# Graph attention on one Trainium2 core: loading x ahead of the edges' numbers, preparing these on POOL, and reordering node work in the turns and at the end

## The chip, the cores and the metric

The kernel runs on one core of a Trainium2 chip. A core has five engines that the profile names: PE (TensorE, matrix products and transposes, with its weight loads listed as PEld), DVE (VectorE), ACT (ScalarE), POOL (GpSimd) and SP (SyncE, which here only issues DMAs). Each takes its instructions strictly in the order of the program, and semaphores make one wait for another. The metric is the time of one execution on the device in microseconds; lower is better.

## The reference

12,500 nodes with 128 features each, and 212,500 edges sorted by their destination `dst`. With 8 heads of 16 features, cut to what matters:

```python
h = maximum(layernorm(x), 0)
q = (h @ Wq.T + bq); k = (edge_h @ Wk.T + bk); v = (h @ Wv.T + bv)   # 8 heads x 16
qs, qd = q[src], q[dst]
in_m, out_m, diag_m = sum(qs * k), sum(qd * k), sum(qs * qd)          # over 16 features
score = (segment_softmax(in_m * 0.25, dst) + segment_softmax(out_m * 0.25, dst)
         + segment_softmax(diag_m * 0.25, dst)) * distance ** lam
h = segment_sum(score[..., None] * v[dst], dst)
return x + leaky_relu(h @ Wo.T + bo, slope=0.1)
```

Since `v[dst]` is the same for all edges of a node, only the three sums of weighted and unweighted exponentials are needed for each node and head; v is multiplied in afterwards, node by node.

## The kernel before, in words

The function is `ordered_path`. It has three stages, all in one program.

**Preparation** (`prep`). x is loaded whole into `xq` (98 tiles of 128 nodes) by nine DMAs in SP's queue. For each group g of four tiles DVE takes statistics (`statistics`, `scale`), ACT normalizes (`rectify`, L863), PE transposes (L870), ACT copies (`hT`, L872), PE multiplies by Wq (L878), DVE adds bq (L881) and SP stores the result to the table `q_table` (L882). Between groups stand pieces of other work, called from the dictionary `side` at a given g: the edges' numbers (`edges_1` to `edges_4`), the transposes of the other weights (`turn_ws`) and the biases' three-term form (`biases`, L822). The edges' numbers are `src`, `dst` and the edge weights, each as 104 rows of 2,048; they are loaded by POOL's queue (`rows_in`, L608 to L610). From src come the transposed integers `src_i`, by which rows are gathered (PE L749, DVE L750); from dst and the weights come bf16 tables in memory: `fa_d` (marks where a segment starts, and three bf16 terms of the weight, written by `fa_out`, L758), `rel_d` (the node's number within a block, L786) and `ends_d`. These share two buffers tagged `of`. After the groups a loop over `terms_q` splits q into three bf16 terms and stores them as `q3_table` (L898 to L907), while POOL begins to gather. The first nine groups of gathers (`gather`, L656) need all of `q_table`. At the end of the stage some small instructions work out a flag (L954 to L978); what follows waits for it.

**The edge loop.** The edges stand in 416 blocks of 512, cut into five strips. One iteration g handles one block; five iterations s = 0 to 4, one for each strip, make a turn t, and there are 84 turns. In an iteration PE, in this order, computes k for block g+1 (`project`, L1115 and L1117), spreads q of the destinations over block g+1 by a one-hot product (`spread_q`, L1126, into the one buffer `qd_ps`), and transposes the features of block g+2 (`turn`, L1107). ACT copies `qd_ps` (L1128) and the transposed features `eT` (L1109) and makes the one-hots of block g+3 (L1101, L1102). DVE forms the products and sums them to logits (`logits`, L1137, L1138, L1140). POOL gathers q of the sources nine blocks ahead. In fixed steps s the preceding turn is handled: its logits are transposed (s=0), scanned for maxima (s=1), turned into powers (s=2: PE L1182, ACT L1183 to L1188), scanned for sums (s=3, DVE L1194 and L1198), its ends shown (s=4, L1214 to L1218), and the sums of the turn before it are transposed (L1226), gathered to rows (L1239) and stored (L1251). The PSUM tiles of these steps come from one tag, `small`, with three buffers in rotation.

**Node work.** Units of 256 nodes whose sums are complete are handled in pairs, 20 of them, each over four turns, by `nodes_between`, which is called as the last thing in an iteration: sums and x loaded, normalized, divided (`scores`), transposed (`turn`), multiplied by Wv (`project_v`: PE L1049 and L1051, then DVE L1059), and two turns later by Wo (`project_o`: PE L1049 and L1051, ACT L1069, DVE L1070 and L1071), and stored. The remaining nine units, `rest`, are five `Nodes` objects; `begin_rest` loads, normalizes, transposes and multiplies them by Wv during the last iterations, and the loop at the end of the function does what needs the last sums: `scores` (whose first addition, L1032, joins two parts of a unit's sums), L1059, the transposes, `project_o` and the store.

Order is written by hand: `pin` makes an instruction follow the one pinned before it on its engine, so each engine's order is that of the Python calls. Buffers and semaphores do the rest.

```python
        side = {2: edges_1, 5: turn_ws, 6: biases, 8: edges_2, 11: edges_3, 14: lambda: edges_4(0),
                17: lambda: edges_4(1), 20: lambda: edges_4(2)}
```

Of the kernel before, what the change touches and what calls it, by code (L numbers as in the profile page):

```python
# [20 lines left out]
SLOPE = 0.1  # L21
# [451 lines left out]
def ordered_path(ctx: ExitStack, tc: tile.TileContext, flag, x, src, dst, edge_attr, edge_weight,  # L473
# [131 lines left out]
    def rows_in(to, t, q):  # L605

        top, cut = (RW - 1) * RC, 96
        q.dma_start(to[0:cut, :], t[:cut * RC].rearrange("(r c) -> r c", c=RC))  # L608
        q.dma_start(to[cut:RW - 1, :], t[cut * RC:top].rearrange("(r c) -> r c", c=RC))
        q.dma_start(to[RW - 1:RW, :E - top], t[None, top:E])  # L610
# [69 lines left out]
    with tc.tile_pool(name="prep", bufs=1) as prep, \  # L680
# [7 lines left out]
        pin(nc.sync.dma_start(w_in[:, 0, :], Wq))  # L688
        xq = prep.tile([P, NI, F], F32, name="xq")
        LOADS = [0, 2, 4] + list(range(CU, NU + 1, CU))  # L690
        for lo, hi in zip(LOADS, LOADS[1:]):
            nodes_in(xq[:, 2 * lo:2 * hi, :], lo, hi - lo, nc.sync)
            if lo == 0:
                pin(nc.sync.dma_start(bq_all, bq[None, :].to_broadcast([P, F])))
        b_row = prep.tile([1, 3, F], F32, name="b_row")
# [15 lines left out]
        src_r = prep.tile([RW, RC], I32, name="src_r", tag="step")  # L711
        nc.gpsimd.memset(src_r[96:, :], 0)
        rows_in(src_r, src, nc.gpsimd)

        dst_r = prep.tile([RW, RC + 2], I32, name="dst_r")
        nc.gpsimd.memset(dst_r[96:, :], N)
        nc.gpsimd.memset(dst_r[:, 0:1], -1)
        rows_in(dst_r[:, 1:RC + 1], dst, nc.gpsimd)
        pin(nc.gpsimd.dma_start(dst_r[1:, 0:1], dst[RC - 1:(RW - 1) * RC:RC, None]))
        pin(nc.gpsimd.dma_start(dst_r[:RW - 1, RC + 1:], dst[RC:(RW - 1) * RC + 1:RC, None]))  # L720
        weight = prep.tile([RW, RC], F32, name="weight")
        nc.gpsimd.memset(weight[96:, :], 1.0)
        rows_in(weight, edge_weight.rearrange("e o -> (e o)"), nc.gpsimd)
# [39 lines left out]

        def edges_1():
            pin(nc.vector.tensor_copy(src_f, src_r))
            turn_edges(src_f, src_i)

        def edges_2():
            pin(nc.gpsimd.tensor_copy(dst_f, dst_r))
            step = got["step"] = prep.tile([RW, RC + 1], F32, name="step", tag="step")  # L770
            pin(nc.vector.tensor_sub(step, dst_f[:, 1:], dst_f[:, :RC + 1]))
            of = of_tile()
            pin(nc.gpsimd.tensor_scalar(of, step[:, :RC], 0.0, -FAR, op0=ALU.is_gt, op1=ALU.mult))
            fa_out(0, of)

        def edges_3():
            base_c = prep.tile([RW, RB], F32, name="base_c")
            pin(nc.vector.tensor_copy(base_c, dst_f[:, 1:RC + 1:BE]))
            for a in range(RB):
                part = rel[:, a * BE:(a + 1) * BE]  # L780
                pin(nc.vector.tensor_scalar(part, part, base_c[:, a:a + 1], 1.0, op0=ALU.subtract,
                                            op1=ALU.add))
            rel_b = of_tile().rearrange("r (a e) -> r a e", a=RB)
            pin(nc.gpsimd.tensor_copy(rel_b.rearrange("r a (j p) -> r a j p", j=JN),
                                      rel.rearrange("r (a p j) -> r a j p", a=RB, j=JN)))
            pin(nc.sync.dma_start(rel_d.rearrange("(r a) e -> r a e", a=RB), rel_b))  # L786

        def edges_4(c):
            of = of_tile()
            pin(nc.gpsimd.tensor_copy(of, weight))  # L790
            if c < 2:
                pin(nc.vector.tensor_sub(weight, weight, of))
            fa_out(c + 1, of)
# [94 lines left out]
        def terms_q(g):  # L888

            if g < GN:  # L890
                n = len(tiles_of(g))
                q = xq[:, g * JN:g * JN + n, :]
                if g % 3 == 2:
                    q3 = prep.tile([P, JN, 3, F], BF, name="q3", tag="of", bufs=2)
                else:
                    q3 = node.tile([P, JN, 3, F], BF, name="q3", bufs=4)
# [13 lines left out]

        side = {2: edges_1, 5: turn_ws, 6: biases, 8: edges_2, 11: edges_3, 14: lambda: edges_4(0),
                17: lambda: edges_4(1), 20: lambda: edges_4(2)}
# [17 lines left out]
        for g in range(-2, GN):  # L930
# [8 lines left out]
            if g in side:  # L939
                side[g]()  # L940
        for g in range(LOOK):
            gather(g)
        for g in range(AHEAD):
            fetch_edges(g)
        fetch(0)
        for g in range(GN + 1):
            terms_q(g)
            if g % 3 == 2:
                edges_5(g // 3)
# [44 lines left out]
    class Nodes:  # L994
# [59 lines left out]
        def project_v(self, to):  # L1054
            self.product(to, bv3, wv)
            self.weigh(to)
# [8 lines left out]
        def project_o(self, to):  # L1065
            n = self.n
            self.product(to, bo3, wo)
            o, y = self.h[:, :n], self.x[:, :n]
            pin(nc.scalar.activation(o, to[:, :n], AF.Copy, scale=SLOPE))  # L1069
            pin(nc.vector.tensor_max(o, o, to[:, :n]))  # L1070
            pin(nc.vector.tensor_add(y, o, y))  # L1071
# [18 lines left out]
    with tc.tile_pool(name="work", bufs=2) as work, \  # L1090
# [167 lines left out]

        def nodes_between(t, s):
# [5 lines left out]
            if new and even and s == 2:  # L1265
                new.normalize(0, 2)
                new.scores()
# [25 lines left out]
        def begin_rest(at):  # L1293
# [4 lines left out]
            for r, (of, begin) in enumerate(zip(rest, starts)):  # L1298
# [23 lines left out]
        for g in range(end + 2 * S):  # L1322
            s, t = g % S, g // S
            if g < end:
# [94 lines left out]
```

## Time and profile before

| | |
|---|---|
| median of 14 runs | 2898.01 us (2885.97 to 2908.07) |
| the profiled execution | 2887.07 us |
| its span in the profile | 2885.3 us |
| mean granted PE clock | 0.706 |
| busy share PE, DVE, ACT, POOL | 69%, 72%, 58%, 57% |
| first gather (POOL, L656) | at 95.02 us |
| first product of the edge loop's logits (DVE, L1137) | at 153.20 us |
| last L1140 | at 2825.81 us |
| last store issued | at 2878.51 us |

The profile's page gives the busy time of each engine, the span in slices, the DMA queues, the chain that ended last, and groups of instructions by source line, with the idle time of the engine in front of each group and what ended it. Further views list instructions in order of time, the waits by pair of waiting and releasing instruction, and the busy time of each engine in chosen windows. Line numbers in the profile before are those of the kernel before.

### The profile page before, as it was taken

How to read it: one execution, taken by the hardware profiler on the slowest of the kernel's cores; microseconds unless marked ns; L12 is line 12 of the kernel's file. 1: busy time of each engine (PE TensorE's matmuls, PEld its weight loads, DVE VectorE, ACT ScalarE, POOL GpSimd, SP SyncE). 2: the span in 40 equal slices, each digit the busy share in tenths (PEclk: the TensorE clock that was granted, in tenths of full speed). 3: DMA queues.
4: the chain of work that ended last, by engine and by line, in shares of the span. 5: the costliest groups of instructions: out<-in, count | busy, mean ns of one | idle time of the engine just before them, and what ended most of it. 6: DMA issues, size and time to landing. Idle time of an engine off the chain costs nothing.

```text
span 2885.3 us, 36583 instructions
## 1 busy us (share of the span) xinstructions
PE 1982.8 (69%) x10781; PEld 1525.0 (53%) x10781; DVE 2087.3 (72%) x2180; ACT 1665.5 (58%) x3049; POOL 1645.3 (57%) x1716
## 2 busy tenths in 40 slices
PE   5256766766667676767677777776767676777676
PEld 4145555555555555555555555555555555555554
DVE  7757776777777777767776777777767777777775
ACT  5645655555555656556555555565555555656573
POOL 4665666666656556556565555656655556555630
PEclk8657766676777767767776667677667677777677
DMA  6853334334343434343443433443433334433431
GB/s 174 272 157 108 112 116 117 109 115 121 109 118 113 121 104 119 114 116 116 118 116 107 121 112 115 125 114 112 118 105 121 108 115 119 122 108 114 118 90 33
DMA packets 308901, 341.93 MB, mean 119 GB/s; under 512 B 139780, under 2 KB 227609, under 8 KB 308382
## 3 DMA queue, kind: packets, MB, share of 16 engines
q1 hardware_dynamic: 246259, 223.55, 26.0%
q0 software_dynamic: 54448, 112.96, 14.0%
q10 hardware_dynamic: 7984, 3.00, 0.4%
q8 instruction: 86, 1.41, 0.2%
q14 instruction: 124, 1.02, 0.1%
HBM read 308.22 MB, written 31.07 MB: 118 GB/s over the span
## 4 chain that ended last, share of the span: by engine, by line
PE 42%; ACT 24%; another core or an unknown queue 13%; issue 10%; DMA 5%; DVE 3%; POOL 1%; SPq 0%; ACTq 0%; POOLq 0%; DVEq 0%
PE k_ps L1117 15%; PE eT_ps L1107 7%; ACT eT L1109 4%; ACT qq L1128 4%; ACT relb L1101 4%; PE qd_ps L1126 4%; ACT oh L1102 4%; PE w_ps L1239 3%; PE b_ps L1226 3%; PE k_ps L1115 3%; PE d_ps L1214 2%; ACT l L1160 2%; DMA qq<-q_table,src_i 2%; ACT sel L1217 2%
## 5 line engine op out<-in xcount | busy, mean ns | idle before, releaser
L656 POOL DMA_INDIRECT qq<-q_table,src_i x1680 | 1608.4, 957 | 1085.5 <-issue 471.3
L1117 PE MATMUL k_ps<-wk,eT 128*128 128x128 f32 x3360 | 677.8, 364 | 621.6 <-ACT eT L1109 296.3
L1117 PEld LDWEIGHTS k_ps<-wk,eT 128*128 128x128 f32 x3360 | 575.0, 258 | 776.9 <-issue 361.5
L1140 DVE TENSOR_REDUCE lT<-prod 128x96 f32<-128x1536 f32 x420 | 736.3, 1753 | 14.3
L1128 ACT COPY qq<-qd_ps 128x512 f32<-128x512 f32 x420 | 244.7, 583 | 598.2 <-PE qd_ps L1126 187.7
L1137 DVE TENSOR_TENSOR prod<-qq,qd_ps 128x512 f32<-128x512 f32 x420 | 285.8, 681 | 386.3 <-ACT qq L1128 197.7
L1138 DVE TENSOR_TENSOR prod<-qq,k_ps 128x1024 f32<-128x1024 f32 x420 | 510.2, 1215 | 0.0
L1109 ACT COPY eT<-eT_ps 128x512 f32<-128x512 f32 x420 | 247.1, 588 | 348.8 <-remote 250.5
L1107 PE MATMUL eT_ps<-ident,ea 128*128 128x128 f32 x1680 | 359.5, 355 | 6.1 <-DVE found L955 5.6
L1101 ACT ACTIVATE relb<-relb,before 126x512 bf16<-126x512 bf16 x420 | 305.9, 728 | 0.0
L1126 PE MATMUL qd_ps<-win,oh 126*128 126x128 bf16 x1680 | 217.9, 270 | 114.9 <-DVE prod L1137 78.1
L1102 ACT ACTIVATE oh<-relb 126x512 bf16<-126x512 bf16 x420 | 264.5, 630 | 23.0 <-DVE flag L978 9.7
L1107 PEld LDWEIGHTS eT_ps<-ident,ea 128*128 128x128 f32 x1680 | 256.1, 189 | 5.9 <-DVE found L955 5.9
L1126 PEld LDWEIGHTS <-oh 126*128 126x128 bf16 x1680 | 171.3, 125 | 143.7 <-DVE prod L1137 79.9
L1226 PE MATMUL b_ps<-ident,sum 120*128 120x120 f32 x672 | 151.6, 364 | 89.2 <-ACT l L1160 63.1
L1115 PE MATMUL k_ps<-b,ones 3*128 3x512 bf16 x420 | 190.9, 454 | 5.1 <-issue 4.5
L1239 PE MATMUL w_ps<-back,sel 128*126 128x144 f32 x1344 | 189.7, 295 | 0.6 <-ACT back L1227 0.6
L1239 PEld LDWEIGHTS w_ps<-back,sel 128*126 128x126 f32 x1344 | 171.4, 190 | 22.9 <-issue 20.5
L1226 PEld LDWEIGHTS b_ps<-ident,sum 120*128 120x128 f32 x672 | 106.1, 215 | 143.3 <-ACT l L1160 81.1
L1070 DVE TENSOR_TENSOR h<-h,node_ps 128x512 f32<-128x512 f32 x20 | 13.8, 688 | 163.8 <-ACT h L1069 154.2
L1227 ACT COPY back<-b_ps 128x480 f32<-128x480 f32 x168 | 96.9, 577 | 48.5 <-PE b_ps L1226 44.4
L1170 DVE TENSOR_TENSOR_SCAN u<-l,u,far_ps 120x512 f32<-120x512 f32 x83 | 105.5, 1271 | 1.9 <-ACT l L1160 1.8
(187 smaller groups left out, 1998.5 us busy)
## 6 DMA issues: line engine op xcount, KB each, us to landing
ea<-in_edge_attr_dram SPq DMA_DIRECT2D x419, 256.0 KB
relb<-rel_d SPq DMA_DIRECT2D x84, 630.0 KB
qq<-q_table,src_i POOLq DMA_INDIRECT x1680
win<-q_table SPq DMA_DIRECT2D x420, 31.5 KB
q_table<-q SPq DMA_DIRECT2D x24, 384.0 KB
fa<-fa_d SPq DMA_DIRECT2D x420, 4.0 KB
sums<-rows SPq DMA_DIRECT2D x416, 7.9 KB
q_table<-xq SPq DMA_DIRECT2D x24, 256.0 KB
```

The lines of the kernel that those rows point to most:

```text
L656: rows = pin(nc.gpsimd.indirect_dma_start(out=qq[:, j, 0, :], out_offset=None, in_=q_table, in_offset=bass.IndirectOffsetOnAxis(ap=src_i[: ...
L1101: pin(nc.scalar.activation(d, d, AF.Abs, bias=before[:K3]))
L1102: pin(nc.scalar.activation(oh, d, AF.Relu, bias=1.0, scale=-1.0))
L1107: pin(nc.tensor.transpose(eT_ps[:, j, :], eas[g][:, j * F:(j + 1) * F], ident))
L1109: pin(nc.scalar.copy(eT, eT_ps))
L1117: pin(nc.tensor.matmul(k_ps[:, j, :], eTs[g][:, j, :], wk, start=False, stop=(j == JN - 1)))
L1126: pin(nc.tensor.matmul(qd_ps[:, j, :], ohs[g][:, j * P:(j + 1) * P], d["win"][:, s, :], start=(j == 0), stop=(j == JN - 1)))
L1128: pin(nc.scalar.copy(qqs[g][:, :, 1, :], qd_ps))
L1138: pin(nc.vector.tensor_mul(prod[:, :, 0:2, :], qqs[g], ks[g][:, :, None, :].to_broadcast([P, JN, 2, F])))
L1140: pin(nc.vector.tensor_reduce(lTs[t][:, :, s, :], prod.rearrange("p j i (h d) -> p j (i h) d", d=DIM), AX.X, ALU.add))
L1226: pin(nc.tensor.transpose(b_ps[:, j, :], d["nd"][i][:, j:BE:JN], ident[:R, :R]))
L1239: pin(nc.tensor.matmul(w_ps[:, i].rearrange("p s c -> p (s c)"), d["sel"][:, j, lo:lo + 3, :].rearrange("p s w -> p (s w)"), d["back"][:, ...
```

## The change

Four things are done. (1) In preparation, src, the weights and dst are loaded by SP's queue after all of x, where POOL's queue loaded them beside x. Their conversion and splitting goes to POOL (`edges_0`, at g = 0), the pieces of the edges' numbers come at later g (9, 15, 18), two of the stores come after the groups (`edges_4`), the first features of edges (`fetch_edges`) are fetched among the groups and the first `fetch(0)` within the loop of `terms_q`, which uses four buffers `q3` for all groups. (2) A new function, `nodes_before`, called first in an iteration, issues the products of `project_v` and `project_o` and ACT's scaled copy; the DVE parts (`weigh`, `add_x`) stay at the end of the iteration. (3) The addition of two parts of sums becomes `add_sums`, on POOL, and the last addition of the remaining units is done on POOL too. (4) In the last iterations the transposes of the last remaining object and of the last pair come later, and so do the products with Wv.

```diff
@@ rows_in: the three DMAs are pinned
@@ preparation
+        src_r = prep.tile([RW, RC], I32, name="src_r", tag="step")
+        nc.gpsimd.memset(src_r[96:, :], 0)
+        weight = prep.tile([RW, RC], F32, name="weight")
+        nc.gpsimd.memset(weight[96:, :], 1.0)
+        dst_r = prep.tile([RW, RC + 2], I32, name="dst_r")
+        nc.gpsimd.memset(dst_r[96:, :], N)
+        nc.gpsimd.memset(dst_r[:, 0:1], -1)
...
             nodes_in(xq[:, 2 * lo:2 * hi, :], lo, hi - lo, nc.sync)
...
+        rows_in(src_r, src, nc.sync)
+        rows_in(weight, edge_weight.rearrange("e o -> (e o)"), nc.sync)
+        rows_in(dst_r[:, 1:RC + 1], dst, nc.sync)
+        pin(nc.gpsimd.dma_start(dst_r[1:, 0:1], dst[RC - 1:(RW - 1) * RC:RC, None]))
+        pin(nc.gpsimd.dma_start(dst_r[:RW - 1, RC + 1:], dst[RC:(RW - 1) * RC + 1:RC, None]))
...
-        rows_in(src_r, src, nc.gpsimd)
...
-        rows_in(dst_r[:, 1:RC + 1], dst, nc.gpsimd)
...
-        rows_in(weight, edge_weight.rearrange("e o -> (e o)"), nc.gpsimd)
...
+        def edges_0():
+            pin(nc.gpsimd.tensor_copy(src_f, src_r))
+            got["weights"] = [of_tile(), of_tile()]
+            for of in got["weights"]:
+                pin(nc.gpsimd.tensor_copy(of, weight))
+                pin(nc.gpsimd.tensor_sub(weight, weight, of))
+            pin(nc.gpsimd.tensor_copy(dst_f, dst_r))
         def edges_1():
-            pin(nc.vector.tensor_copy(src_f, src_r))
             turn_edges(src_f, src_i)
+            step = got["step"] = prep.tile([RW, RC + 1], F32, name="step", tag="step")
+            pin(nc.gpsimd.tensor_sub(step, dst_f[:, 1:], dst_f[:, :RC + 1]))
         def edges_2():
-            pin(nc.gpsimd.tensor_copy(dst_f, dst_r))
...
-            pin(nc.vector.tensor_sub(step, dst_f[:, 1:], dst_f[:, :RC + 1]))
+            for c, of in enumerate(got["weights"]):
+                fa_out(c + 1, of)
             of = of_tile()
+            pin(nc.gpsimd.tensor_copy(of, weight))
+            fa_out(3, of)
         def edges_3():
+            of = got["cuts"] = of_tile()
+            pin(nc.gpsimd.tensor_scalar(of, got["step"][:, :RC], 0.0, -FAR, op0=ALU.is_gt, op1=ALU.mult))
...
+        def edges_4():
+            fa_out(0, got["cuts"])
+            pin(nc.sync.dma_start(rel_d.rearrange("(r a) e -> r a e", a=RB), got["rel_b"]))
...
-                if g % 3 == 2:
-                    q3 = prep.tile([P, JN, 3, F], BF, name="q3", tag="of", bufs=2)
...
+        side = {0: edges_0, 4: turn_ws, 6: biases, 9: edges_1, 15: edges_2, 18: edges_3}
...
+            if 9 <= g < 9 + AHEAD:
+                fetch_edges(g - 9)
         for g in range(LOOK):
             gather(g)
-        for g in range(AHEAD):
-            fetch_edges(g)
-        fetch(0)
+        edges_4()
         for g in range(GN + 1):
             terms_q(g)
+            if g == 3:
+                fetch(0)
@@ class Nodes
+        def add_sums(self):
+            for ab, more in self.more:
+                pin(nc.gpsimd.tensor_add(ab, ab, more))
         def scores(self):
-            for ab, more in self.more:
-                pin(nc.vector.tensor_add(ab, ab, more))
...
         def project_v(self, to):
+            self.held = to
             self.product(to, bv3, wv)
-            self.weigh(to)
...
         def project_o(self, to):
             self.product(to, bo3, wo)
+            o = self.h[:, :n]
+            self.held = to
+            pin(nc.scalar.activation(o, to[:, :n], AF.Copy, scale=SLOPE))
+        def add_x(self, engine):
+            n, to = self.n, self.held
             o, y = self.h[:, :n], self.x[:, :n]
-            pin(nc.scalar.activation(o, to[:, :n], AF.Copy, scale=SLOPE))
             pin(nc.vector.tensor_max(o, o, to[:, :n]))
-            pin(nc.vector.tensor_add(y, o, y))
+            pin(engine.tensor_add(y, o, y))
@@ the edge loop
+        def nodes_before(t, s):
+            new, old = pairs.get(t - t % 2), pairs.get(t - t % 2 - 2)
+            if new and t % 2 == 1 and s == 4:
+                new.project_v(small([P, JN, F], "node_ps"))
+            if old and t % 2 == 0 and s == 4:
+                old.project_o(small([P, JN, F], "node_ps"))
@@ nodes_between
+                new.add_sums()
                 new.scores()
...
-                new.project_v(small([P, JN, F], "node_ps"))
-            if old and even and s == 1:
+                new.weigh(new.held)
+            if old and even and s == (1 if t < T else 2):
                 old.turn(small([P, JN, P], "node_ps"))
             if old and even and s == 4:
-                old.project_o(small([P, JN, F], "node_ps"))
+                old.add_x(nc.vector)
@@ begin_rest
-                if at == begin + 3:
+                if at == (begin + 3 if r < 4 else LOOK + 3):
...
-                if at == LOOK + r:
+                if at == LOOK + (3, 4, 7, 7, 7)[r]:
@@ the loop over g, and the end
+            nodes_before(t, s)
             if g < end:
                 gather(g + LOOK)
...
+        for of in rest:
+            of.add_sums()
...
                 rest[r - 2].project_o(small([P, JN, F], "node_ps"))
+                rest[r - 2].add_x(nc.gpsimd)
                 rest[r - 2].store()
```

More of the change, by code (lines that the diff above doesn't have):

```diff
@@ L607, in rows_in @@
         top, cut = (RW - 1) * RC, 96
-        q.dma_start(to[0:cut, :], t[:cut * RC].rearrange("(r c) -> r c", c=RC))
-        q.dma_start(to[cut:RW - 1, :], t[cut * RC:top].rearrange("(r c) -> r c", c=RC))
-        q.dma_start(to[RW - 1:RW, :E - top], t[None, top:E])
+        pin(q.dma_start(to[0:cut, :], t[:cut * RC].rearrange("(r c) -> r c", c=RC)))
+        pin(q.dma_start(to[cut:RW - 1, :], t[cut * RC:top].rearrange("(r c) -> r c", c=RC)))
+        pin(q.dma_start(to[RW - 1:RW, :E - top], t[None, top:E]))
     qqs, st, eas, behind, base_v = {}, {}, {}, {}, {}
@@ L709, in ordered_path @@
         pin(nc.sync.dma_start(tops[:, T - 1:, S - 1:S], dst[None, E - 1:E, None]))
-        src_r = prep.tile([RW, RC], I32, name="src_r", tag="step")
-        nc.gpsimd.memset(src_r[96:, :], 0)
-        rows_in(src_r, src, nc.gpsimd)
-        dst_r = prep.tile([RW, RC + 2], I32, name="dst_r")
-        nc.gpsimd.memset(dst_r[96:, :], N)
-        nc.gpsimd.memset(dst_r[:, 0:1], -1)
-        rows_in(dst_r[:, 1:RC + 1], dst, nc.gpsimd)
[L719 to L722, printed above, removed]
-        rows_in(weight, edge_weight.rearrange("e o -> (e o)"), nc.gpsimd)
         for i, w in enumerate((Wv, Wk, Wo)):
@@ L762, in of_tile @@
             return prep.tile([P, RC], BF, name="of", bufs=2)[:RW]
+        def edges_0():
[5 more added lines that the diff above has]
+            pin(nc.gpsimd.tensor_copy(dst_f, dst_r))
         def edges_1():
-            pin(nc.vector.tensor_copy(src_f, src_r))
             turn_edges(src_f, src_i)
+            step = got["step"] = prep.tile([RW, RC + 1], F32, name="step", tag="step")
+            pin(nc.gpsimd.tensor_sub(step, dst_f[:, 1:], dst_f[:, :RC + 1]))
         def edges_2():
-            pin(nc.gpsimd.tensor_copy(dst_f, dst_r))
-            step = got["step"] = prep.tile([RW, RC + 1], F32, name="step", tag="step")
-            pin(nc.vector.tensor_sub(step, dst_f[:, 1:], dst_f[:, :RC + 1]))
+            for c, of in enumerate(got["weights"]):
+                fa_out(c + 1, of)
             of = of_tile()
-            pin(nc.gpsimd.tensor_scalar(of, step[:, :RC], 0.0, -FAR, op0=ALU.is_gt, op1=ALU.mult))
-            fa_out(0, of)
+            pin(nc.gpsimd.tensor_copy(of, weight))
+            fa_out(3, of)
         def edges_3():
+            of = got["cuts"] = of_tile()
+            pin(nc.gpsimd.tensor_scalar(of, got["step"][:, :RC], 0.0, -FAR, op0=ALU.is_gt, op1=ALU.mult))
             base_c = prep.tile([RW, RB], F32, name="base_c")
@@ L782, in edges_3 @@
                                             op1=ALU.add))
-            rel_b = of_tile().rearrange("r (a e) -> r a e", a=RB)
+            rel_b = got["rel_b"] = of_tile().rearrange("r (a e) -> r a e", a=RB)
             pin(nc.gpsimd.tensor_copy(rel_b.rearrange("r a (j p) -> r a j p", j=JN),
                                       rel.rearrange("r (a p j) -> r a j p", a=RB, j=JN)))
[L786 to L793, printed above, removed]
+        def edges_4():
+            fa_out(0, got["cuts"])
+            pin(nc.sync.dma_start(rel_d.rearrange("(r a) e -> r a e", a=RB), got["rel_b"]))
         def edges_5(i):
@@ L892, in terms_q @@
                 q = xq[:, g * JN:g * JN + n, :]
-                if g % 3 == 2:
-                    q3 = prep.tile([P, JN, 3, F], BF, name="q3", tag="of", bufs=2)
-                else:
-                    q3 = node.tile([P, JN, 3, F], BF, name="q3", bufs=4)
+                q3 = node.tile([P, JN, 3, F], BF, name="q3", bufs=4)
                 q3 = q3s[g] = q3[:, :n]
@@ L909, in terms_q @@
                     q3.rearrange("p (u k) t f -> p u (k t f)", k=2)))
-        side = {2: edges_1, 5: turn_ws, 6: biases, 8: edges_2, 11: edges_3, 14: lambda: edges_4(0),
-                17: lambda: edges_4(1), 20: lambda: edges_4(2)}
+        side = {0: edges_0, 4: turn_ws, 6: biases, 9: edges_1, 15: edges_2, 18: edges_3}
         turn_w(0, wq)
```

## Prediction

> **What bounds the kernel now.** I read the page first, then its stages by windows, then the waits and the timeline of the places that the diff touches.
>
> The page: no engine is full over the span, so what one stage or one wait costs has to be read from that stage.
>
> ```profile
> PE 1982.8 (69%) x10781; PEld 1525.0 (53%) x10781; DVE 2087.3 (72%) x2180; ACT 1665.5 (58%) x3049; POOL 1645.3 (57%) x1716
> ...
> L1070 DVE TENSOR_TENSOR h<-h,node_ps 128x512 f32<-128x512 f32 x20 | 13.8, 688 | 163.8 <-ACT h L1069 154.2
> ```
>
> The second line is the oddest of the page: 20 instructions of 0.69 us, with 163.8 us of idle DVE in front of them. Windows by stage:
>
> ```profile
> 24.40:39.00 14.60, 4.24 (x23) 3.87 (x23) 9.65 (x36) 1.13 (x4) 1.51 (x1) 0.61 0.88 248
> ...
> 59.00:66.00 7.00, 3.38 (x19) 3.19 (x18) 6.90 (x25) 0.55 (x2) 6.29 (x1) 0.74 0.07 25
> 66.00:88.20 22.20, 20.56 (x125) 16.70 (x126) 15.84 (x23) 21.98 (x56) 10.35 (x5) 0.87 0.74 224
> ...
> 95.00:132.40 37.40, 1.98 (x6) 0.89 (x6) 31.58 (x49) 22.82 (x42) 30.98 (x22) 0.50 0.90 308
> 132.40:144.10 11.70, 0.00 (x0) 0.02 (x1) 4.59 (x20) 1.94 (x4) 9.19 (x9) 0.50 0.54 183
> 144.10:2826.00 2681.90, 1888.75 (x10290) 1451.24 (x10290) 1955.55 (x1833) 1565.09 (x2829) 1568.56 (x1651) 0.71 0.40 115
> 2826.00:2854.80 28.80, 20.59 (x112) 16.03 (x112) 8.57 (x9) 10.19 (x20) 0.00 (x0) 0.80 0.10 26
> 2854.80:2885.30 30.50, 15.16 (x59) 10.86 (x59) 17.99 (x46) 5.48 (x10) 0.00 (x0) 0.56 0.18 52
> ```
>
> (Columns: window, length, busy PE, PEld, DVE, ACT, POOL with counts, granted clock, DMA share, GB/s.) Preparation is 0 to 144, the edge loop 144 to 2826, the end 59 us. In preparation ACT stands still twice (24.4 to 39, 59 to 66) in a stage that it fills at 66 to 88. The reductions of the logits (L1140), counted by windows, show what node work costs the loop:
>
> ```profile
> 180.00:780.00 600.00, 168.31 (x96) 0.71 0.40 117
> 780.00:2680.00 1900.00, 517.16 (x295) 0.70 0.40 115
> ```
>
> An iteration takes 600/96 = 6.25 us before the first pair of units and 1900/295 = 6.44 after it. One pair in the timeline, and the waits of 700 to 2700:
>
> ```profile
> 809.62 0.58 ACT L1109 COPY eT<-eT_ps 128x512 f32<-128x512 f32 x1 [3.67 <-remote]
> ...
> 813.15 0.58 ACT L1069 ACTIVATE h<-node_ps 128x512 f32<-128x512 f32 x1
> ...
> 813.76 0.69 DVE L1070 TENSOR_TENSOR h<-h,node_ps 128x512 f32<-128x512 f32 x1 [8.94 <-ACT h L1069]
> ...
> 815.83 0.61 PE L1126 MATMUL qd_ps<-win,oh 126*128 126x128 bf16 x4 [3.49 <-DVE prod L1137]
> ```
>
> ```profile
> PE qd_ps L1126 <- DVE prod L1137: 74.4, 19, 6.6
> ```
>
> DVE stands at L1070 behind ACT's whole turn (the copy eT, the one-hots, three sel), its next logits start at 815.09, and PE, which has one buffer qd_ps, waits 3.5 us for them. That last wait occurs 19 times, 74.4 us: this is where node work gets onto the path. The end:
>
> ```profile
> 2835.54 0.63 ACT L1183 ACTIVATE up<-gap 120x512 f32<-120x512 f32 x1
> ...
> 2837.65 0.69 DVE L1194 TENSOR_TENSOR ew<-up,att_ps 120x512 f32<-120x512 f32 x1 [5.70 <-PE att_ps L1182]
> ...
> 2844.96 1.12 PE L1226 MATMUL b_ps<-ident,sum 120*128 120x120 f32 x8
> ```
>
> **The change, part by part.**
>
> *Preparation.* Removed from POOL's queue: nine row loads (0.5 to 0.7 us each); put on SP's: the same nine, behind x and ahead of the biases, bases and tops and of every q_table write. The bytes are the same 9.3 MB (225 x 12 + 239 x 12.4 + 248 x 14.6), so at 240 GB/s they still take until about 39 us; but x, 6.4 MB, is complete near 28, and the 16 transposes of src no longer stand ahead of the node work on PE, which waited 10.4 us for them (L749 <- DVE src_r). ACT's period per group of four tiles is 2.02 us where it runs free (hT copies at 71.57, 73.59, 75.61); 27 rounds from 12 us, with 2.1 us for seven inv and 0.8 us for the three weights, end near 70 instead of 88. DVE, relieved of src_f (1.23), step (2.27) and two weight differences (2 x 2.29), 8.1 us, has some 56 us of work in these 58, so it binds about as much: say 72. SP's small loads (eleven at 0.75 us) end near 48 as now (45), so the q_table writes start with a backlog: 6.4 MB, with 1.5 MB of ea now between them and 1.3 MB of fa, 9.2 MB at 300 GB/s are done near 79, not 94. From there 9.6 MB of q3 and the first gathers; the 308 GB/s of 95 to 132 is the limit seen, and the whole 30 MB moved by 132.4 would take 39 us + 20.7 MB at 300 GB/s = 108 at the earliest. With four q3 buffers for six, and with SP standing at relb until rel_d and fa have landed (one landing, 2 to 3 us), I put the end of that stage at 116: 16 us gained. The 11.7 us of flags behind it stay. Bounds: 6 (if writes and loads only change places) and 24.
>
> Here a rule speaks against the change. The trace has no two-input operation on POOL; its rows for 104x2048 are a cast at 1.89 us and a two-step tensor_scalar at 7.12, DVE's difference takes 2.29. The Trainium skill, GPSIMD Engine Reference, section Engine selection, says to keep elementwise arithmetic on VectorE, and its section Performance versus the Vector engine gives 4.5 us on GPSIMD against 2.3 for this very size. POOL now has, after src lands near 31: four casts (7.6), three differences, one more cast (1.9), 7.1, 3.9. With 4.5 us each, an estimate from that page, that is 34 us, done near 70 with waits; with 7.1 each (the dear row) 42 us, near 78. Both end before q_table is written (79), so I charge nothing for the length; if that cover goes, gathers and with them the 9 groups of lookahead shift one to one, at most some 3 us. The page also says that the two engines contend for SBUF when DVE has two SBUF inputs. The trace agrees in one place: L840, 0.17 us elsewhere, took 1.33 under POOL's L773. Some three such meetings are 3 us of a DVE that now binds; they are in the 72.
>
> biases (L822) now comes at round 6 and waits for b_row behind dst, 39 us; DVE's work before it also takes until about 39, so nothing, with the q_ps additions and all statistics queued behind it if b_row is late (1 us for 1).
>
> *Loop.* 20 pairs: L1049/L1051 of project_v and project_o go ahead of project(g+1) on PE, L1069 ahead of qq(g+1) on ACT; L1059, L1070, L1071 stay last on DVE, so logits(g) and the pair of node operations no longer wait for ACT's turn. Nothing is added: PE 1.55 us (0.39 + 1.16) at the full clock or 2.7 (0.63 + 2.08) at half, ACT 0.58, DVE 0.69 x 3. What goes is at most the 3.9 us of PE's wait per pair (74.4/19), 78 us; by the windows 0.19 us x 295 = 56 us for the 19 pairs in them. What is late next: the copy eT at 809.62, which DVE does not govern (ACT waits 4.4 us for it at 682.85 as well, where no node work is), and PE, for the product now delays k_ps and qd. In front of project PE mostly waits anyway for ACT's eT (200.0 us over 57 waits), and the product's PSUM buffer comes free with ew (L1194), 1.1 us before project started in the turn at 800. I take 2.1 us per pair: 42 us, with 20 to 65 as this case's own ends. add_sums on POOL concerns no pair (each has one part).
>
> *End.* rest[4]'s and the last pair's transposes move behind the powers, so up (L1183) can follow gap, 2831.94, at once, not at 2835.54: 3.6 us. Sums then end near 2837, and b_ps no longer stands behind three of five products (2844.85): together 7 us. The three products now run while rows are stored and sums loaded (2849.0 to 2854.8). Behind that DVE sheds six L1032 (0.2) and five L1071 (0.7), 5 us, but PE, ACT and the maximum chain on: by hand the last maximum comes 4.1 us earlier and the last addition, half size on POOL, takes some 0.6 for 0.42 us, leaving 3.5. Together 10.5, bounds 4 and 14.
>
> Sum: 16 + 42 + 10.5 = 68.5 us off the profiled execution's 2887.1 (span 2885.3 and 1.8 around it), 2818.6. The median of 14 runs is 2898.0, 0.38% above that execution: 2829.
>
> **The rivals.** *Loop without gain:* the eT copy that ends the stall is not DVE's to give, and the product takes back what the freed DVE gives; preparation and end alone, 26.5 us: 2871. For: the same stall at 682.85. Against: PE's 74.4 us name DVE. Chance 0.15. *Slower:* the product ahead of project delays k_ps, qd and the logits in 40 turns without DVE's wait being saved; place: PE at L1117, price 1.55 to 2.7 us each. It outweighs preparation and end from 26.5/40 = 0.66 us; at 1.55 it costs 62: 2934. At a quarter of that it is the first rival again. For: PE is 69% busy at a clock of 0.7. Chance 0.12. *DMA-bound preparation:* the same bytes, one queue, 16 us become nothing: 2845. For: share 0.88 and 0.90 in both stages. Chance 0.13. *All of it:* the loop gives 65 to 78 us, preparation 24, end 14: 103 to 116, 2790. Chance 0.12. That all cancels within 0.2% (6 us, about what can be told from no change here): 0.03. My forecast as summed: 0.45.
>
> The range 2785 to 2888 takes in all cases but the slower one, the tie and part of the last. Faster 0.85, same 0.03, slower 0.12.
>
> **What would show it.** L1070's successor with under 20 us of idle DVE before it, and PE's wait for DVE prod at qd_ps gone: the loop's step. If those go and the reductions still come every 6.44 us, the first rival holds; if they come every 6.6 or more, the slower one. First gather near 80 instead of 95 and first logits near 137 instead of 153: preparation. Rows' last store (2849.4) to the end of DVE as now less 3.5, and up within 1 us of gap: the end. Wrong altogether if PE's k_ps waits grow by over 60 us.

## The result, and the profile after

The changed kernel takes 2814.2 us (median of 10 runs, 2806.0 to 2817.4) where the kernel before takes 2897.6 (47 runs, 2880.3 to 2919.4): ratio 0.9706, interval [0.9687, 0.9725], 83.4 us faster. The forecast was 2829 us, 69 us faster. The number came out nearly right, its three terms did not. The profiled execution has a span of 2812.1 us against 2885.3, 73.2 us less; the other 10 us of the medians' difference are that the profiled execution of the kernel before lay 10.5 us under its median, and that of the changed kernel at its own.

The first line of the page after, and the group of DVE's maximum (L1082, L1070 before) in the turns:

```profile
PE 1927.9 (69%) x10781; PEld 1505.3 (54%) x10781; DVE 2096.1 (75%) x2165; ACT 1659.2 (59%) x3049; POOL 1670.9 (59%) x1722
...
L1082 DVE TENSOR_TENSOR h<-h,node_ps 128x512 f32<-128x512 f32 x20 | 13.6, 678 | 2.6 <-ACT h L1077 2.6
```

The idle time before the twenty maxima is 2.6 us where it was 163.8. The windows of the stages (columns as before: window, length, busy PE, PEld, DVE, ACT, POOL, clock, DMA share, GB/s), cut where the changed kernel's stages end:

```profile
24.40:42.40 18.00, 14.04 (x96) 11.24 (x94) 17.69 (x75) 15.63 (x42) 7.92 (x4) 1.00 0.58 136
42.40:60.00 17.60, 2.48 (x13) 2.48 (x14) 16.54 (x34) 0.69 (x2) 8.57 (x4) 0.59 0.52 165
60.00:91.00 31.00, 25.00 (x159) 20.74 (x158) 19.69 (x24) 25.16 (x64) 15.48 (x4) 0.89 0.59 184
...
96.10:141.20 45.10, 1.98 (x6) 0.89 (x6) 34.55 (x51) 24.52 (x45) 37.57 (x25) 0.51 0.82 268
141.20:147.30 6.10, 0.01 (x1) 0.04 (x1) 4.64 (x20) 1.83 (x4) 4.79 (x5) 0.50 0.64 215
147.30:2753.20 2605.90, 1838.62 (x10288) 1435.11 (x10289) 1959.91 (x1832) 1557.10 (x2825) 1574.80 (x1652) 0.74 0.41 118
2753.20:2777.50 24.30, 19.23 (x115) 15.12 (x114) 8.76 (x9) 11.76 (x23) 0.00 (x0) 0.93 0.12 32
2777.50:2812.10 34.60, 12.54 (x59) 9.12 (x59) 14.73 (x35) 5.48 (x10) 7.98 (x11) 0.68 0.15 46
```

The first line shows that the wait for x is gone: DVE is busy for 17.69 of 18 us. The second is a standstill of another kind: DVE is busy for 16.54 of 17.6 us with only 34 instructions, while ACT does two. The stage of the terms takes 45.1 us (37.4 before). And the reductions, now L1152:

```profile
180.00:780.00 600.00, 168.67 (x97) 0.71 0.40 116
780.00:2680.00 1900.00, 537.81 (x307) 0.75 0.42 120
```

600/97 and 1900/307 are both 6.19 us: an iteration with node work costs no more than one without.

With the starts of the first and the last reduction as marks, both traces split into three parts:

| | before | after | difference | predicted |
|---|---|---|---|---|
| to the first reduction | 155.06 | 152.67 | -2.4 | -16 |
| first to last reduction | 2670.76 | 2600.53 | -70.2 | -42 |
| last reduction to the end | 59.46 | 58.89 | -0.6 | -10.5 |

So the loop brought nearly everything, and two of three terms nearly nothing. The experiments ask why, and they turned up something larger: the 70 us are not a property of the kernel alone.

### The profile page after: what moved, and what is told of

Its sections match the earlier page's. It is cut to its first block, busy times and chain, and to the rows that moved or that the text cites. A ratio compares the mean times of both kernels' runs of the same rounds, so it can differ in the third digit from the quotient of the medians.

```text
span 2812.1 us, 36553 instructions
## 1 busy us (share of the span) xinstructions
PE 1927.9 (69%) x10781; PEld 1505.3 (54%) x10781; DVE 2096.1 (75%) x2165; ACT 1659.2 (59%) x3049; POOL 1670.9 (59%) x1722
## 5 line engine op out<-in xcount | busy, mean ns | idle before, releaser
L1129 PE MATMUL k_ps<-wk,eT 128*128 128x128 f32 x3360 | 686.3, 367 | 582.2 <-ACT eT L1121 371.4
L1129 PEld LDWEIGHTS k_ps<-wk,eT 128*128 128x128 f32 x3360 | 582.8, 261 | 742.5 <-ACT eT L1121 429.8
L1152 DVE TENSOR_REDUCE lT<-prod 128x96 f32<-128x1536 f32 x420 | 736.3, 1753 | 14.3
L1119 PE MATMUL eT_ps<-ident,ea 128*128 128x128 f32 x1680 | 352.0, 349 | 3.1 <-issue 2.1
L1238 PE MATMUL b_ps<-ident,sum 120*128 120x120 f32 x672 | 141.1, 342 | 141.9 <-issue 72.3
L1210 DVE TENSOR_TENSOR_SCAN sum<-keep,sum,up 120x512 f32<-120x512 f32 x83 | 106.0, 1277 | 0.0
```

The costliest lines, as they stand in the source:

```text
L1119: pin(nc.tensor.transpose(eT_ps[:, j, :], eas[g][:, j * F:(j + 1) * F], ident))
L1129: pin(nc.tensor.matmul(k_ps[:, j, :], eTs[g][:, j, :], wk, start=False, stop=(j == JN - 1)))
L1152: pin(nc.vector.tensor_reduce(lTs[t][:, :, s, :], prod.rearrange("p j i (h d) -> p j (i h) d", d=DIM), AX.X, ALU.add))
L1238: pin(nc.tensor.transpose(b_ps[:, j, :], d["nd"][i][:, j:BE:JN], ident[:R, :R]))
```

## The experiments

Ten kernels ran, on three chips: A (experiments 1, 2, 6 and 7), B (3, 4 and 8) and C (5). On A and B the kernel before takes 2292.6 and 2293.7 us, on C 2901.2 us, like the runs of the result. A and B are called the fast kind below, C and the chip of the result the slow kind; each chip was used in one stretch of time only, so a lasting property of a chip and a passing one are not told apart. Every ratio is to the kernel before on the same chip. No trace of the kernel before was taken on A or B, and the changed kernel itself ran on B, not on A or C.

**1. The loop alone** (chip A). From the kernel before, only this (cut to what matters):

```diff
+            nodes_before(t, s)
...
-                new.project_v(small([P, JN, F], "node_ps"))
+                new.weigh(new.held)
...
-                old.project_o(small([P, JN, F], "node_ps"))
+                old.add_x(nc.vector)
```

> The kernel before, with only the node work of the turns reordered (products and the scaled copy first in a turn, DVE's part last); preparation and end as before. Theory A (read from the stage boundaries of the two traces): the loop alone carries the gain. First to last reduction falls from 2670.8 us to about 2600 us, preparation and end stay at 155 and 59.5 us, the time is about 2897.6 - 70 = 2827 us. Rival B (the sum of the prediction): the loop is worth 42 us and the rest comes from the other two parts, so about 2855 us here.

Measured: 2288.8 us against 2292.6, ratio 0.9976 [0.9962, 0.9989]. The whole program is 600 us shorter than in the profile of the result, and the reordering is worth 0.24%, 4 us by the medians. Neither theory expected that, and it does not decide between them.

**2. Preparation of the kernel before, loop and end of the changed one** (chip A): the text of the kernel before down to the end of `prep`, the changed text from there.

> The changed kernel with the preparation of the kernel before: loop and end are the changed ones. Theory A: the changed preparation is worth only what its end shows, 155.1 - 152.7 = 2.4 us, so undoing it costs 2.4 us: about 2816.5 us, first gather near 95, first reduction near 155. Rival B (preparation worth 16 us): about 2830 us.

Measured: 2289.9 us, ratio 0.9981 [0.9970, 0.9991]; first gather at 93.66, first reduction at 140.9. The forecasts were for the slow kind and cannot be read here. Experiment 1 has the same preparation, and there these two stand at 97.23 and 147.06: single traces of one text can lie 6 us apart.

**3. The changed kernel again** (chip B), because of these two.

> The changed kernel as it is, again, since the first four runs stood on a chip where the kernel before takes 2292.6 us and not 2897.6 us. Theory A (the 83 us depend on late semaphore arrivals: in the traces of 2885 and 2812 us all engines stand still together for over 0.5 us some 80 times in the loop, in the four traces of 2281 to 2289 us three to five times): where the kernel before takes about 2290 us, this one gains 3 to 8 us, ratio 0.997; where it takes about 2900 us, it gains about 83, ratio 0.971. Rival B (each of the four variants lost most of the gain by what it undid): ratio 0.97 on any chip.

Measured: 2296.1 us against 2293.7, ratio 1.0011 [0.9999, 1.0023]. Where the kernel before takes 2293 us, the change that saves 83 us elsewhere saves nothing. Rival B falls; Theory A's point, that the gain depends on the chip, holds, though its small gain did not come: with experiment 2 beside it, the changed preparation costs about 0.3% (7 us) here, which the loop's 0.24% cannot cover. (That is a comparison over two chips, but the intervals [0.9970, 0.9991] and [0.9999, 1.0023] don't meet.)

Why the two kinds differ can be seen in part: a handover, by which one engine's semaphore update lets the next engine go on, comes late. One line, the register step ahead of the five stores of rows (min/median/max ns): before in the result's profile, then the changed kernel on chip B:

```profile
L1251 SPq MOVE sums<-rows x416: 2/17/1407, 246.9 to 2851.4; - x139
```

```profile
L1263 SPq MOVE sums<-rows x416: 29/29/38, 222.1 to 2257.9; - x139
```

A step that takes 29 ns on chip B takes up to 1407 in the result's trace. Of SP's 840 such steps, 149 to 164 take over 0.5 us in each of the five traces of the slow kind; in the seven of the fast kind the longest is 43 ns. The idle time of ACT before the copy eT, again before and on chip B:

```profile
  remote: 250.5, 79
```

```profile
  PE eT_ps L1119: 40.9, 156
```

In the first, ACT waits 250.5 us in 79 places for an update that the trace cannot place. Before 105 of the 420 copies ACT stands idle for over 1 us after PE's transposes have ended; in the seven traces of the fast kind before none. On chip B its waits there are 0.26 us long on average, each ended by PE. Intervals of over 0.5 us, between the first and the last reduction, in which PE, DVE and ACT all stand still: 79 before and 86 after (139.0 and 143.1 us), 50 to 69 in the three traces of chip C, 3 to 6 in those of the fast kind. So on chips of the slow kind handovers between engines come late, on the others not.

What makes them late is not settled, nor whether they are the whole difference. The loop of the changed kernel takes 2600.5 us in the result and 2082.8 on chip B; the standstills are 143 of the 518 us between them. The granted clock is lower as well, 0.706 to 0.741 in the traces of the slow kind against 0.793 to 0.812, and PE is busy in this loop for 1834.8 us against 1718.2. In preparation the changed kernel gets nearly the same clock on both (1.00 and 1.00 from 24.4 to 42.4 us, 0.51 and 0.50 from 96 to 141), so the lower clock may follow from PE's waiting in the loop and not cause it; no run here tests that. The consequence for DVE is plain; windows within the loop of the kernel before (result's trace) and of the changed kernel on chip B:

```profile
700.00:2700.00 2000.00, 1424.55 (x7750) 1093.83 (x7750) 1460.90 (x1386) 1170.58 (x2117) 1179.18 (x1242) 0.71 0.40 115
```

```profile
600.00:2100.00 1500.00, 1243.78 (x7452) 952.33 (x7452) 1391.96 (x1329) 1115.81 (x2034) 1136.86 (x1191) 0.81 0.53 147
```

DVE is busy for 73% of the first and for 93% of the second. On chip B it is close to the bound: an iteration takes 2082.81/419 = 4.97 us, and an order that frees DVE from waits has almost no waits to free. Its waits there:

```profile
ACT qq L1140 <- PE qd_ps L1138: 258.5, 170, 4.1
...
PE qd_ps L1138 <- DVE prod L1149: 158.0, 110, 3.8
...
DVE prod L1149 <- DMA qq<-q_table,src_i: 57.8, 38, 4.6
```

PE and ACT wait, in turn, for DVE; DVE itself waits for gathers.

**4. DVE's part first as well** (chip B): `add_x` called from `nodes_before`, and `weigh` likewise.

```diff
                 old.project_o(small([P, JN, F], "node_ps"))
+                old.add_x(nc.vector)
```

> The changed kernel, with DVE's part of the node work (weigh, maximum, addition) also first in the iteration, right behind PE's and ACT's part, so that DVE again waits for ACT before it can go on with the logits. Theory A (the loop's gain is DVE's freedom from that wait): DVE idles before the maximum again, some 4 to 8 us for each of 40 turns, and most of the gain of the loop goes: about 2855 to 2885 us where before takes 2898, about 2290 to 2310 where before takes 2293. Rival B (the gain is the place of PE's product, ahead of the projection): the time stays that of the changed kernel, within 5 us.

Measured: 2298.0 us, ratio 1.0015 [0.9999, 1.0032], the changed kernel within 2 us. Inconclusive: both theories allowed this where before takes 2293 us, since on this chip neither order shows a cost.

**5. ACT made late once a turn** (chip C), as a test of whether lateness on ACT's chain is what made the old order dear. Into three kernels go eight more operations of ACT (the kernel before; the loop alone as in 1; and a third order):

```diff
+            if s == 4 and g + 2 < end:
+                for i in range(8):
+                    pin(nc.scalar.activation(late_out[i % 2], late_in, AF.Relu, bias=1.0, scale=-1.0))
             if g + 2 < end:
                 turn(g + 2)
```

The kernel before:

> The kernel before, with ACT made late once a turn: in iteration s = 4, ahead of the copy eT, eight more operations of 0.52 us on a scratch tile, 4.2 us, as that copy came 4 to 5 us late in the trace of 2885 us. The results are those of the kernel before. Theory A (late handovers on ACT's chain are what made the old order of node work dear): in the 40 turns with a product DVE stands at the maximum or at the weighing behind ACT's longer turn, s = 4 of those turns takes 12 us or more, and the time is 2293 + 84 x 1.5 to 4 + 40 x 2 us or more, 2500 to 2700 us. The number that counts is the distance to the next kernel. Rival B (it is something else in that trace that made the old order dear): the next kernel is as slow as this one, within 10 us.

The loop reordered as in the change:

> The same eight operations in the kernel before with only the node work of the turns reordered. Theory A: DVE is free of ACT's longer turn, so that this kernel is 40 to 80 us faster than the one before it, against 4 us without the eight operations (2288.8 to 2292.6). Rival B: the distance stays below 10 us.

Product and scaled copy last as before the change, DVE's part one iteration later:

> As the kernel before this one, with PE's product and ACT's scaled copy at the old place (last in the iteration, behind the eight operations) and DVE's weigh, maximum and addition one iteration later. Theory A (what counts is that DVE's part stands an iteration behind ACT's): as fast as the kernel before it, within 10 us. Rival C (what counts is that the product and the copy come first on PE and ACT): as slow as the first of the three, within 10 us.

The chip turned out to be one on which the kernel before takes 2901.2 us, so the lateness was added to what was there, and the first forecast, counted from 2293 us, missed. Measured: 2968.0, 2951.7 and 2912.8 us; ratios 1.0223 [1.0190, 1.0256], 1.0172 [1.0146, 1.0198], 1.0037 [1.0010, 1.0065]. The changed order is 0.5%, 16 us, better than the old one (six runs of each, and the two intervals just overlap): between Theory A's 40 to 80 and Rival B's 10, so neither came true. The third order is 39 us better still. That refutes Rival C (front place needed), and Theory A's "within 10 us" missed as well. The waits of 700 to 2700 show where the expected gain of the second went; first the kernel before with ACT late, then the changed order:

```profile
DVE h L1070 <- ACT h L1069: 168.6, 17, 12.1
...
DVE prod L1137 <- ACT qq L1128: 144.2, 83, 6.3
DVE h L1059 <- remote: 117.9, 17, 10.2
...
ACT qq L1128 <- remote: 63.9, 14, 6.9
```

```profile
DVE prod L1144 <- ACT qq L1135: 408.7, 156, 5.6
...
ACT qq L1135 <- remote: 242.7, 45, 7.7
```

DVE's wait for ACT's node copy, 168.6 us, and the 117.9 before the weighing are gone, but ACT waits 179 us more before the copy qq, and DVE behind it 265 us more before its products. With the product first, ACT's scaled copy stands ahead of qq, and the product on PE ahead of k; the likely reading is that a late handover there passes through qq to DVE, but no run moved the two apart. In the third order:

```profile
DVE prod L1144 <- ACT qq L1135: 197.6, 99, 5.7
ACT qq L1135 <- remote: 111.5, 24, 7.6
...
DVE h L1077 <- ACT h L1072: 70.3, 14, 5.7
```

So, with ACT made late, the iteration between ACT's part and DVE's is what pays, and the place ahead of the projection has a price of its own. The clock does not explain this order: the second kernel has the highest, 0.735 against 0.711 and 0.719, and not the shortest time. Whether the third order beats the changed one on this chip without the added lateness was not tried.

**6. The biases moved** (chip A), a test of preparation. In the changed kernel's trace POOL's splitting of the weights stands beside DVE's small instructions (timeline: start, duration, engine, line):

```profile
38.20 4.08 POOL L770 TENSOR_TENSOR weight<-weight,of 104x2048 f32<-104x2048 f32 x1
...
42.34 1.92 POOL L769 CAST of<-weight 104x2048 bf16<-104x2048 f32 x1
...
42.45 1.85 DVE L850 SCALAR_TENSOR_TENSOR sums<-sums 128x14 f32<-128x14 f32 x1
...
44.34 4.08 POOL L770 TENSOR_TENSOR weight<-weight,of 104x2048 f32<-104x2048 f32 x1
44.43 4.19 DVE L829 CAST terms<-b_row 1x384 bf16<-1x384 f32 x1
...
57.52 1.66 PE L749 MATMUL t_ps<-ident,src_r 104*128 104x104 f32 x8 [15.84 <-DVE src_i L750]
```

The cast L829 took 0.35 us in the kernel before; here it starts 0.09 us after POOL's difference and ends 0.2 us after it. DVE's queue slips, and PE waits 15.84 us for the copy to `src_i` that stands in it.

```diff
-        side = {0: edges_0, 4: turn_ws, 6: biases, 9: edges_1, 15: edges_2, 18: edges_3}
+        side = {0: edges_0, 4: turn_ws, 9: edges_1, 12: biases, 15: edges_2, 18: edges_3}
```

> The changed kernel with one move: the four small DVE operations of the biases stand at round 12 of preparation, not at round 6, so that they no longer run beside POOL's splitting of the weights. Nothing is added or removed. Theory A (POOL's long operations hold DVE's instructions that read SBUF): the first two bias operations take 0.35 and 0.55 us, not 4.19 and 2.12; PE's wait of 15.84 us for the copy to src_i falls below 10; the node rounds end some 5 us earlier, first gather near 91, time about 2809 us. Rival B (the transfers bind preparation, whatever DVE does): first gather stays at 96, time 2814 us, within 2.

Measured: 2286.3 us, ratio 0.9970 [0.9954, 0.9987], first gather at 91.01, first reduction at 147.69. In the four traces with the changed preparation as it is (the result's, experiments 3, 4 and 7) the gather stands at 96.08 to 96.93 and the reduction at 152.67 to 154.11. PE's wait for `src_i` is 9.7 us. The line of the cast now (min/median/max ns):

```profile
L829 DVE CAST terms<-b_row x1: 337/337/337, 59.9 to 59.9; 1x384 bf16<-1x384 f32 x1
```

Theory A holds: with the same work and bytes, preparation is 5 to 6 us shorter, by one trace against four that lie 1.4 us apart.

**7. The last additions back on DVE** (chip A).

```diff
-                rest[r - 2].add_x(nc.gpsimd)
+                rest[r - 2].add_x(nc.vector)
```

> The changed kernel with the last additions of the remaining units on DVE as before; only the sums are still added on POOL. Theory A: POOL's closing work (a 2.09 us step and a drain of 7.83 us after POOL's last instruction) lies on the path only because POOL has the last addition; with POOL done some 18 us earlier the drain is hidden, and last reduction to end falls from 58.9 to 52 to 54 us, the time to about 2809 us. Rival B (the landing of the last stores sets the end): 58.9 stays, within 1, time 2814 us.

Measured: 2287.5 us, ratio 0.9974 [0.9961, 0.9987]; last reduction to end 54.93 us against 58.89 and 59.25 in the two traces of the changed kernel. Theory A holds in its cause, with 4 us for its 5 to 7. POOL's closing drain, first in the changed kernel, then here (min/median/max ns, first and last start):

```profile
L1439 POOLq DRAIN  x3: 46/103/7831, 2803.4 to 2811.8; - x3
```

```profile
L1439 POOLq DRAIN  x3: 46/103/7831, 2261.1 to 2283.1; - x3
```

The long drain takes 7.83 us in both. In the first it starts at 2803.4, behind POOL's last addition, and the program ends 0.9 us after it; in the second it starts 22 us before the end and is hidden.

**8. The changed kernel mended** (chip B): biases as in 6, the end as in 7, POOL's 7.12 us operation (`cuts`) in four pieces at round 9, each table stored as its tile is ready, six buffers q3.

```diff
+            for a in range(0, RC, BE):
+                pin(nc.gpsimd.tensor_scalar(of[:, a:a + BE], step[:, a:a + BE], 0.0, -FAR, op0=ALU.is_gt, op1=ALU.mult))
...
+                if g % 3 == 2:
+                    q3 = prep.tile([P, JN, 3, F], BF, name="q3", tag="of", bufs=2)
```

> The changed kernel mended where its trace shows loss: biases at round 12; the marks of the segments' starts made on POOL right after step, in four pieces, so that they no longer run beside DVE's four subtractions; each store of these tables as soon as its tile is ready; six buffers for the three-term tiles as before; the last additions of the remaining units on DVE. Theory A: DVE's four subtractions take 0.5 us each (8.6 us together in the changed kernel), first gather near 86 to 88 instead of 96, the stage of terms some 37 instead of 45 us, first reduction near 135 to 140, end 54.9 instead of 58.9: 15 us less than the changed kernel. Rival B (the transfers take back what DVE gives): first reduction stays near 148 to 153, and only the end's 4 us are gained.

Measured: 2276.9 us against 2293.7 before and 2296.1 for the changed kernel on the same chip; ratio to before 0.9930 [0.9911, 0.9949]. First gather at 84.49, first reduction at 133.24, end 56.1. DVE's four subtractions beside POOL's operation in the changed kernel, and in the mended one:

```profile
L792 DVE TENSOR_SCALAR dst_r<-dst_r,base_c x4: 471/478/7374, 78.8 to 86.9; 104x512 f32<-104x512 f32 x4
```

```profile
L793 DVE TENSOR_SCALAR dst_r<-dst_r,base_c x4: 483/484/490, 71.7 to 72.9; 104x512 f32<-104x512 f32 x4
```

One of the four waited out the 7.12 us; now none does. Rival B falls: the first reduction stands 21 us earlier than in the changed kernel on the same chip (154.11), and the program is 19 us shorter where Theory A said 15. Five things changed at once here, so what each brought is shown only for those of experiments 6 and 7. This version beats both kernels on chip B. On a chip of the slow kind it did not run.

## Why the prediction was right in its number, point by point

**The loop, -42 predicted, -70.2 measured.** The mechanism was right: L1082 has 2.6 us of idle DVE before it, and PE's wait for DVE at qd_ps, 74.4 us in the window and 78.1 over the program, is 3.1 us over the program after. The term that was mis-sized is the choice of 2.1 us per pair out of at most 3.9. Measured is 70.2/20 = 3.5, and the 70.2 lie above the end of 65 that I gave. I had held 1.8 us back for a late eT copy and for the product's delay of k; but turns without node work (3 to 17) are about as long as before, 31.17 against 30.96 us, and turns 20 to 79, with 18 pairs in them, take 30.95 us each where they took 32.17.

The product did delay something. My own sign of failure, "wrong altogether if PE's k_ps waits grow by over 60 us", occurred, and the kernel was 83 us faster all the same. The waits of DVE from 700 to 2700 before, then waits of three engines after:

```profile
DVE h L1070 <- ACT h L1069: 147.4, 17, 10.8
...
DVE prod L1137 <- ACT qq L1128: 111.9, 75, 4.9
DVE h L1059 <- remote: 86.4, 14, 9.7
```

```profile
DVE prod L1149 <- ACT qq L1140: 286.4, 125, 6.5
PE k_ps L1129 <- ACT eT L1121: 279.9, 76, 9.9
ACT qq L1140 <- remote: 227.7, 44, 6.9
```

PE's wait for eT grew by 80 us (from 200.0), ACT's before qq by 186 (from 41.3), DVE's behind it by 175 (from 111.9), while more iterations passed in the same 2,000 us (PE's 8042 instructions for 7750). DVE's account over the whole loop, first to last reduction, shows why this was no loss in sum. Its idle time before the first product grew from 376.0 to 570.6 us, but 159.3 us before the maximum and 117.8 before the weighing went to nothing; in all it fell from 717.2 to 642.4 us. These 75 us, less 5 us more of work, are the loop's gain of 70.2. The weighing's wait is not in the prediction's working, which priced PE's wait at qd_ps. The test had to be the period of the reductions, which the text named too.

What the prediction did not see is that the 70 us belong to the slow kind of chip, where handovers come late. It read 73% busy DVE as a fact of the kernel, and noticed the eT copy's 4.4 us at 682.85 without asking why the copy came so long after PE. On chips A and B the loop is worth 0.24% alone (experiment 1), and the whole change nothing (experiment 3).

**Preparation, -16 predicted, -2.4 measured.** x arrived early and DVE became the bound, as written. The 2.4 us themselves are hardly more than the scatter: in the four traces of the slow kind with the old preparation (before, and experiment 5) the first reduction stands at 153.02 to 155.06. The step that failed is "Some three such meetings are 3 us of a DVE": the meetings of DVE with POOL's long operations cost 17.4 us beyond their usual durations: 6.9 in the four L792, 5.4 in two of the biases' operations, 3.9 in two L847 and one L850, 1.2 in L859 and L789. In the kernel before, two meetings (L840 and L852) cost 2.6. POOL's difference itself was estimated well: 4.5 us, and 4.08 measured. Its length was the wrong question: certain instructions of DVE that began beside it ended only when it had ended. The Trainium skill says so more sharply than the sentence that the prediction used: SBUF — State Buffer, section Who interferes with whom, has an instruction that takes the shared pair of ports hold it for its whole length and the other block fully, and names casts, tensor_scalar and operations with two SBUF inputs. The trace agrees (7.37 us for an L792 beside 7.12 of POOL; 4.19 for a cast beside 4.08), and so do the instructions with at most one SBUF input, which it excepts: fourteen statistics L842 took 2.79 us beside POOL's difference as they did at 13.83 us without it, and the additions L888, whose other input is in PSUM, took 0.69 at most.

The estimate of POOL done near 70 fell too. Its third cast of the weights waited for a table's store to free a buffer, 13.82 us, and SP stood 7.58 us for that cast with the q_table writes behind it:

```profile
71.92 7.58 SPq L758 DMA_DIRECT2D fa_d<-of  x3
...
76.75 1.89 POOL L782 CAST of<-weight 104x2048 bf16<-104x2048 f32 x1 [13.82 <-DMA fa_d<-of]
...
78.75 7.12 POOL L787 TENSOR_SCALAR of<-step 104x2048 bf16<-104x2048 f32 x1
78.78 8.56 DVE L792 TENSOR_SCALAR dst_r<-dst_r,base_c 104x512 f32<-104x512 f32 x4
```

The prediction had counted bytes on SP's queue, but not the wait of the third of three stores. So the last q_table write came at 94, not 79, and the first gather at 96.08, 1 us later than before. With four buffers q3 the terms then ended 8.7 us later (last at 140.90, not 132.21). That the first reduction is 2.4 us earlier all the same comes from the step behind it: 11.8 us from there to the first reduction, 22.9 before. That last gain is again one of the slow chips: on chip A the old preparation needs 11.2 and 11.3 us for it, on chip C 20 to 23. The rival "DMA-bound preparation" had the right size (0) for a wrong reason: experiments 6 and 8 shorten the stage with the same bytes.

**The end, -10.5 predicted, -0.6 measured.** Its parts: from the last reduction to the first use of the late sums 29.03 us before, 24.32 after, so -4.7 where I said -7. Up follows gap at once, as forecast:

```profile
2758.62 0.69 DVE L1185 TENSOR_TENSOR gap<-u,l 120x512 f32<-120x512 f32 x1
...
2759.34 0.63 ACT L1195 ACTIVATE up<-gap 120x512 f32<-120x512 f32 x1 [0.68 <-DVE gap L1185]
```

but b_ps (2767.67) still stood behind products with Wv and Wo on PE. From there to the end of the last addition 23.59 before, 21.78 after, so -1.8 where I said -3.5. And from the last addition to the end 6.84 before, 12.79 after: +6.0 where I had no term at all. The prediction priced POOL's addition (0.6 us; 0.73 measured) and not what POOL does once it has done its last: a step of 2.1 us and the drain of 7.83. In the kernel before these lay at 2810 to 2821, under other work, and nothing in a list of waits pointed at it. Experiment 7 shows it.

**The sum.** -2.4, -70.2 and -0.6 make the 73.2 us. Two terms too large by 23.5 and one too small by 28.2 came out within 5 us of the sum, and that is luck; 10 us more came from where the profiled execution of before lay under its median. The rival "slower" (product ahead of k, 1.55 us in 40 turns) found its wait in the trace but not its price; "loop without gain" is near to what happens on chips A and B, where DVE is busy for about nine tenths.

## What to carry to other kernels

An order that takes waits away is worth what the waits are worth on the chip at hand: here, where DVE was busy for 93% of the loop, next to nothing, and where it was busy for 73%, 70 us. Before moving elementwise work to POOL, list which DVE instructions will run beside it: a cast, a tensor_scalar or an operation with two SBUF inputs could last as long as POOL's whole operation here (7.37 us for 0.48, 4.19 for 0.35). Cut POOL's operation in pieces or move the small ones away. And look at an engine's last instruction: work put on an engine that had long finished also moves that engine's closing steps to the end.

## What the runs showed of the hardware that was not expected

- Two kinds of chips, for one and the same kernel: 2292.6 and 2293.7 us on two, 2901.2 and 2897.6 on the others, with the difference in the loop (for the changed kernel an iteration of 4.97 against 6.2 us), hardly in preparation (its first reduction at 154.11 and 152.67 us). On the slow kind register steps on SP last up to 1.4 us where they last 43 ns at most on the other, and before 105 of the 420 copies eT of the kernel before ACT stood idle for over 1 us after PE had ended. Traces show the lateness, not its source.
- Added lateness is partly free there: eight operations a turn, some 350 us of ACT, cost the kernel before 67 us. ACT's wait before eT, there already, fell from 176.5 us (the result's trace) to 31.4 (remote, 700 to 2700). The third order with these operations is 12 us above the kernel before without them; how long it takes without them is not known.
- After POOL's last work come a step of 2.1 us and a drain of 7.83 us in the six traces with the changed preparation (mended or not), 2.15 and 8.08 us in the six with the old one.
- A cast of one row of 384 elements took 4.19 us on DVE (0.35 elsewhere) beside a difference on POOL of 4.08 us.
